# Maxima over partitions by a transpose, a batch norm chain on GpSimd, and weight steps spaced anew in a convolution and attention kernel

## The chip, the cores and the metric

The kernel runs on one core of a Trainium2 chip. A core has a matrix engine (TensorE, PE in the profile; its weight loads are PEld), three engines for element-wise work (VectorE, DVE; ScalarE, ACT; GpSimd, POOL), and a queue engine (SyncE, SP) that issues the transfers here. Each engine works through its own stream of instructions in order, and the streams meet at semaphores. The metric is the device time of one execution in microseconds; lower is better.

## What is computed

The input is x of shape (128, 128, 16, 16), in float32. Layer 0 is a residual block of two quantised convolutions, layer 1 a bidirectional state-space layer and a mixture of experts. The change lies in layer 0:

```python
def _weight_quant(w):                       # 4 bits
    t = jnp.tanh(w)
    t = t / (2.0 * jnp.max(jnp.abs(t))) + 0.5
    return 2.0 * _quantize_k(t, 4) - 1.0
h = _act_quant(_bn(x, gamma1, beta1))       # clip to 0..1, round to 4 bits
out = _conv3x3(h, _weight_quant(w1) * pat1)
out = _act_quant(_bn(out, gamma2, beta2))
out = _conv3x3(out, _weight_quant(w2) * pat2)
return out + x
```

Here x is first group-normalised. `_bn` takes mean and variance of each channel over the whole batch, so the second convolution can't begin before the first has ended for all images. `jnp.max` runs over the whole weight tensor. The pattern `pat1` leaves five of nine taps, a cross, and `pat2` five others, the diagonals.

## The kernel before, in words

Channels lie on the 128 partitions. Images go two at a time, so there are 64 tiles of 128 x 512 (NP = 64). Four stages follow each other.

*Normalisation* (L346 to L474): all 64 tiles of x are loaded once and stay in SBUF (`xr`). VectorE and ScalarE take statistics of each image, and a chain of small VectorE operations makes scale and bias of group norm and first batch norm (`sc1`, `bi1`).

*First convolution* (`conv1`, L477): for each tile, `quantised` makes the 4-bit image: ScalarE (L488) does the scaling with a clip at zero for one image of the pair, GpSimd for the other (L490, and L492 for the clip, every third of which is VectorE's); on six tiles ScalarE does both. VectorE rounds into a padded buffer (L183, `hpad`, four of them, so the stage prepares tiles up to three ahead). TensorE does five matmuls of 512 columns (L210), ScalarE moves the result out of PSUM (L505), VectorE takes statistics (L506), and all but five tiles (`kept`) are stored to HBM (L508).

*Crossover* (L515 to L523): the statistics are aggregated (L516) and turned into scale and bias of the second batch norm (`sc2`, `bi2`). The helper `rsqrt_eps` adds epsilon on VectorE (L124) and takes the power on GpSimd (L127).

*Second convolution* (`conv2`, L532): each tile is fetched (L544), scaled (L548), rounded (L183) and convolved (L210); GpSimd or, for one image of every second pair, ScalarE (L576, L578) scales the residual, VectorE adds it (L579), TensorE transposes the sum into tokens (L557), ScalarE copies that out (L559), and it is stored (L560).

After that come layers 1 and 2, from L590 on, which neither the change nor the steps of the prediction touch.

The weights of a convolution are quantised by `conv_weights` (L132), a generator: each `next` does one step of some 128 x 1152 elements. It needs a maximum over all partitions twice: once of the tanh values (L138, L141), and once (L161, L163) of what is left after a cast to bfloat16, which tells whether one bfloat16 part is enough. Both are `partition_all_reduce` on GpSimd. The answer goes to `how` (L169). `by_weights` (L215) loads `how` into a register of every engine and branches: to a form with nine taps and three parts, one with nine taps and one part, or one with five taps and one part. With these inputs the last one runs, in both convolutions. The steps for the first convolution are spread through the normalisation; those for the second through the loop of the first convolution, one step at every fifth tile from the eighth (L509), with the rest after the loop (L512).

`second_weights` (L299) is another such generator: it prepares weights of the later layers, among them 16 small copies (L326), four products (L328), two centrings of 128 x 512 (L308, L309) and a 512 KB load (L302). `conv2` calls it at every eighth tile.

Instructions are written in the order of the program, but a scheduler orders each engine's stream by priority; `issue_after` ties the instructions of its block behind the one named. Where it is absent, a step whose inputs are ready may be placed far ahead of where it was written.

Of the kernel before, what the change touches and what calls it, by code (L numbers as in the profile page):

```python
# [8 lines left out]
F32 = mybir.dt.float32  # L9
BF16 = mybir.dt.bfloat16  # L10
AF = mybir.ActivationFunctionType
ALU = mybir.AluOpType
AX = mybir.AxisListType

P = 128
NT = 256
EPS = 1e-5
# [3 lines left out]
SCALE = 225.0  # L21
NLEV = 15.0
# [10 lines left out]

@with_exitstack
def kernel(ctx: ExitStack, tc: tile.TileContext, a: dict):
    from concourse import bass_isa

    nc = tc.nc
    x_d, out_d = a["x"], a["out"]
# [89 lines left out]

    CROSS, DIAGONAL = [1, 3, 4, 5, 7], [0, 2, 4, 6, 8]  # L130

    def conv_weights(parts, how, setup, w, pat, taps, tag):  # L132

        t = setup.tile([P, 9, P], F32, name=f"t_{tag}", tag="t")
        nc.scalar.activation(t, w, AF.Tanh)
        yield
        mx = setup.tile([P, 1], F32, name=f"mx_{tag}", tag="mx")
        nc.vector.tensor_reduce(mx, t, AX.XY, ALU.max, apply_absolute_value=True)  # L138
        yield
        am = setup.tile([P, 1], F32, name=f"am_{tag}", tag="am")  # L140
        nc.gpsimd.partition_all_reduce(am, mx, P, bass_isa.ReduceOp.max)  # L141
        yield
        nc.vector.tensor_scalar(am, am, 2.0, None, ALU.mult)
        rm = setup.tile([P, 1], F32, name=f"rm_{tag}", tag="rm")
        nc.vector.reciprocal(rm, am)
        nc.vector.tensor_scalar(t, t, rm, 0.5, ALU.mult, ALU.add)
        yield
        nc.vector.tensor_scalar(t, t, NLEV, MAGIC, ALU.mult, ALU.add)
        yield
        nc.vector.tensor_scalar(t, t, MAGIC, 2.0, ALU.subtract, ALU.mult)  # L150
        yield
        nc.vector.scalar_tensor_tensor(
            w, t, -NLEV, pat.unsqueeze(2).to_broadcast([P, 9, P]), ALU.add, ALU.mult
        )
        yield
        nc.scalar.copy(parts[:, :, 0, :], w)
        yield
        nc.vector.tensor_tensor(t, w, parts[:, :, 0, :], ALU.subtract)
        yield

        nc.vector.tensor_reduce(mx, t, AX.XY, ALU.max, apply_absolute_value=True)  # L161
        yield
        nc.gpsimd.partition_all_reduce(am, mx, P, bass_isa.ReduceOp.max)  # L163
        yield
        nc.vector.tensor_scalar(am, am, 0.0, 2.0, ALU.not_equal, ALU.mult)
        for tap in range(9):
            if tap not in taps:
                nc.vector.scalar_tensor_tensor(am, pat[:, tap : tap + 1], 0.0, am, ALU.not_equal, ALU.max)
        nc.vector.tensor_copy(how, am)  # L169
        nc.scalar.copy(parts[:, :, 1, :], t)  # L170
        nc.gpsimd.tensor_tensor(w, t, parts[:, :, 1, :], ALU.subtract)
        nc.scalar.copy(parts[:, :, 2, :], w)
# [161 lines left out]
    with tc.tile_pool(name="w1p", bufs=1) as w1p:  # L334
# [15 lines left out]
        with tc.tile_pool(name="setup1", bufs=1) as setup, tc.tile_pool(  # L350
# [1 line left out]
        ) as psa:  # L352
            w1 = w1p.tile([P, 9, P], F32, name="w1", tag="w")
            nc.sync.dma_start(w1, a["L0_conv_w1"])
            weights = conv_weights(wq1, how1, w1p, w1, pat1, CROSS, "c1")
            for _ in range(3):
                next(weights)

# [118 lines left out]
        def conv1(taps, nq):  # L477
            with tc.tile_pool(name="pb", bufs=3) as pb, tc.tile_pool(
                name="psb", bufs=4, space=PSUM
            ) as psb:  # L480
                weights = conv_weights(wq2, how2, w1p, w2, pat2, DIAGONAL, "c2")

                def quantised(i):
                    q = pb.tile([P, 2, NT], F32, name=f"q1_{i}", tag="q", bufs=4)
                    for k in range(2):
                        sc, bi = sc1[:, 2 * i + k : 2 * i + k + 1], bi1[:, 2 * i + k : 2 * i + k + 1]
                        if k == 0 or i % 10 == 5:
                            nc.scalar.activation(q[:, k, :], xr[i][:, k, :], AF.Relu, bias=bi, scale=sc)  # L488
                        else:
                            nc.gpsimd.tensor_scalar(q[:, k, :], xr[i][:, k, :], sc, bi, ALU.mult, ALU.add)  # L490
                            eng = nc.vector if i % 3 == 0 else nc.gpsimd
                            eng.tensor_scalar(q[:, k, :], q[:, k, :], 0.0, None, ALU.max)  # L492
                    quantise(q, hpads[i % 4], nq)

                pads(nq)
                less = offsets(pb, psb, wq1, taps, nq)
                for i in range(3):
                    quantised(i)
                for i in range(NP):
                    if i + 3 < NP:  # L500
                        quantised(i + 3)
                    ps = psb.tile([P, 2, NT], F32, name=f"cv1_{i}", tag="cv")
                    conv3x3(ps, hpads[i % 4], wq1, taps, nq)
                    o1 = kept[i] if i in kept else pb.tile([P, 2, NT], F32, name=f"o1_{i}", tag="o1")
                    nc.scalar.activation(o1, ps, AF.Identity, bias=less)  # L505
                    behind = nc.vector.bn_stats(o1st[:, i, :], o1.rearrange("p b s -> p (b s)"))  # L506
                    if i not in kept:
                        nc.sync.dma_start(o1_d[i], o1)  # L508
                    if i > 5 and i % 5 == 3:  # L509
                        with tc.issue_after(behind.ins):  # L510
                            next(weights, None)
                for _ in weights:  # L512
                    pass

                mv2 = pb.tile([P, 2], F32, name="mv2", bufs=1)  # L515
                nc.vector.bn_aggr(mv2, o1st)  # L516
                rs2 = pb.tile([P, 1], F32, name="rs2", bufs=1)
                nc.vector.tensor_scalar(rs2, mv2[:, 1:2], 1.0 / SCALE**2, None, ALU.mult)
                rsqrt_eps(rs2, rs2, EPS)
                nc.vector.tensor_scalar(sc2, rs2, gam2, 1.0 / NLEV, ALU.mult, ALU.mult)  # L520
                tmp2 = pb.tile([P, 1], F32, name="tmp2", bufs=1)
                nc.vector.tensor_tensor(tmp2, mv2[:, 0:1], sc2, ALU.mult)
                nc.vector.scalar_tensor_tensor(bi2, bet2, NLEV, tmp2, ALU.mult, ALU.subtract)  # L523


        kepts = ExitStack()
# [5 lines left out]
    def conv2(taps, nq):  # L532
        with tc.tile_pool(name="pc", bufs=6) as pc, tc.tile_pool(
# [32 lines left out]
            for i in range(NP):  # L566
# [5 lines left out]
                conv3x3(ps, hpads[i % 4], wq2, taps, nq)  # L572
                for k in range(2):
                    sc, bi = ares[:, b + k : b + k + 1], bres[:, b + k : b + k + 1]
                    if k == 0 and i % 2 == 1:
                        nc.scalar.activation(xr[i][:, k, :], xr[i][:, k, :], AF.Identity, bias=bi, scale=sc)  # L576
                    else:
                        nc.gpsimd.tensor_scalar(xr[i][:, k, :], xr[i][:, k, :], sc, bi, ALU.mult, ALU.add)  # L578
                nc.vector.scalar_tensor_tensor(xr[i], ps, less, xr[i], ALU.add, ALU.add)  # L579

                stored(i - 1)
                if i % max(NP // 8, 1) == 0:
                    next(weights, None)
            stored(NP - 1)
            for _ in weights:
                pass
# [617 lines left out]
```

## Time and profile before

| | us |
|---|---|
| time, median of three runs | 2788.83 |
| lowest and highest | 2786.76, 2788.87 |
| span of the profiled execution | 2784.6 |

The span divides as follows, with the busy time of each engine in each stretch, in microseconds.

| stage | from, to | length | PE | DVE | ACT | POOL |
|---|---|---|---|---|---|---|
| normalisation | 0, 77.77 | 77.77 | 5.2 | 58.0 | 42.8 | 14.8 |
| first convolution, first to last matmul | 77.77, 189.53 | 111.76 | 88.0 | 80.3 | 77.8 | 76.3 |
| crossover | 189.53, 203.08 | 13.55 | 0.3 | 8.4 | 5.6 | 5.3 |
| second convolution | 203.08, 320.15 | 117.07 | 115.3 | 76.7 | 90.6 | 55.5 |
| later layers | 320.15, 2784.6 | 2464.45 | 2407.2 | 2109.6 | 1805.5 | 1492.6 |

How to read the profile. A line of a timeline gives the start, the length, the engine, the source line and operation, the tensors and their shapes, the number of instructions merged in it, and in brackets how long the engine had been idle before it, with what ended that wait ("issue": nothing that the profile shows). L-numbers are lines of the kernel. A code such as 128x512 is partitions by elements. The lines of busy shares cut the span into 40 equal slices and give tenths. The two `partition_all_reduce` calls in the first convolution are the lines L141 and L163; the profile gives them 0.38 us each, and custom operations of GpSimd are recorded roughly.

### The profile page before, as it was taken

The numbers are of one execution on the slowest core, as the hardware profiler recorded it, in microseconds if no ns is written. First come the engines' busy times: TensorE is split into PE (matmuls) and PEld (weight loads), VectorE is DVE, ScalarE is ACT, GpSimd is POOL, SyncE is SP. The second block draws the span as 40 slices with busy tenths as digits, with TensorE's granted clock in tenths as the row PEclk, the third lists the DMA queues.
The fourth block names the chain that finished last, engine by engine and source line by source line (L and its number), as shares of the span: only waits on it lengthen the run. The fifth ranks groups of instructions, "written<-read, shape, count | busy, mean of one in ns | idle before, by whom it ended". The sixth has DMA issues, their size and how long they took to land.

```text
span 2784.6 us, 47424 instructions
## 1 busy us (share of the span) xinstructions
PE 2616.0 (94%) x15840; PEld 1667.9 (60%) x15840; DVE 2333.0 (84%) x6226; ACT 2022.2 (73%) x3538; POOL 1644.5 (59%) x1709
## 2 busy tenths in 40 slices
PE   0769679999999999999999999999999999999997
PEld 0225346666666666666666666666666666666664
DVE  7677589888888888898888888888888898888874
ACT  5659577777777777777777777777777777777771
POOL 1667314666566666665665666656666666566566
PEclk9989889999999999999999999999999999999998
DMA  8348501222222232222222222322222222222223
GB/s 269 119 149 283 180 20 55 89 90 93 86 88 78 85 93 86 92 87 88 81 81 86 93 85 93 93 85 84 81 87 93 86 92 86 88 77 79 85 86 106
DMA packets 165415, 275.55 MB, mean 99 GB/s; under 512 B 46240, under 2 KB 89248, under 8 KB 165152
## 3 DMA queue, kind: packets, MB, share of 16 engines
q1 hardware_dynamic: 165152, 272.32, 30.7%
q8 instruction: 131, 2.15, 0.3%
q14 instruction: 132, 1.08, 0.1%
HBM read 197.45 MB, written 58.03 MB: 92 GB/s over the span
## 4 chain that ended last, share of the span: by engine, by line
PE 87%; POOL 1%; ACT 1%; DVE 1%; DMA 1%; issue 1%; POOLq 0%; ACTq 0%; DVEq 0%; SPq 0%
PE f_ps L1079 16%; PE x_ps L794 12%; PE y_ps L918 9%; PE z_ps L837 9%; PE o_ps L967 8%; PE sg L883 4%; PE n_ps L947 4%; PE y_ps L924 4%; PE xt_ps L849 4%; PE g_ps L868 4%; PE dt_ps L704 2%; PE rt_ps L996 2%; PE cv L210 2%; PE sg L885 2%; PE u_ps L686 1%; PE r_ps L754 1%
## 5 line engine op out<-in xcount | busy, mean ns | idle before, releaser
L893 ACT ACTIVATE e<-sg 128x512 f32<-128x512 f32 x768 | 450.2, 595 | 355.6 <-PE sg L883 317.9
L1067 POOL TENSOR_TENSOR gb<-gb,u2T 128x512 f32<-128x512 f32 x512 | 642.4, 1277 | 7.7 <-DMA gb<-gd 7.7
L812 DVE SCALAR_TENSOR_TENSOR xc<-x_ps,cw,xc 128x510 f32<-128x510 f32 (+2 forms) x768 | 569.3, 741 | 82.2 <-ACT xc L806 74.1
L934 POOL TENSOR_TENSOR yg<-yg,z 128x512 f32<-128x512 f32 x256 | 328.0, 1282 | 447.4 <-DVE yg L930 445.5
L1079 PE MATMUL f_ps<-gb,ew 128*128 128x512 f32 x1024 | 522.3, 604 | 5.9 <-POOL gb L1067 5.7
L794 PE MATMUL x_ps<-uT,wx 128*128 128x512 f32 x768 | 404.7, 609 | 7.7 <-DVE bc L812 3.1
L812 DVE SCALAR_TENSOR_TENSOR bc<-x_ps,cw,bc 128x510 f32<-128x510 f32 (+2 forms) x384 | 281.5, 733 | 126.0 <-ACT bc L806 122.5
L918 PE MATMUL y_ps<-e,xt 128*64 128x256 f32 x2048 | 317.7, 389 | 1.1 <-DVE yg L930 1.1
L899 DVE TENSOR_TENSOR e<-e,g_ps 128x1024 f32<-128x1024 f32 x256 | 310.1, 1211 | 2.0 <-ACT e L893 2.0
L837 PE MATMUL z_ps<-uT,wz 128*128 128x512 f32 x512 | 274.5, 618 | 1.4 <-ACT z L841 1.4
L967 PEld LDWEIGHTS o_ps<-wo,yg 128*128 128x128 f32 x2048 | 239.2, 192 | 17.8 <-issue 17.5
L967 PE MATMUL o_ps<-wo,yg 128*128 128x128 f32 x2048 | 249.8, 275 | 0.0
L1079 PEld LDWEIGHTS f_ps<-gb,ew 128*128 128x128 f32 x1024 | 172.7, 192 | 122.0 <-issue 99.7
L841 ACT ACTIVATE z<-z_ps 128x512 f32<-128x512 f32 x256 | 153.3, 599 | 123.1 <-PE z_ps L837 121.3
L806 ACT ACTIVATE xc<-x_ps,cb,cw 128x512 f32<-128x512 f32 x256 | 198.8, 777 | 44.0 <-PE x_ps L794 41.4
L667 POOL TENSOR_TENSOR rstdb<-rstdb,mhalf 128x4 f32<-128x4 f32 x64 | 64.5, 1007 | 280.9 <-DVE rstdb L664 280.9
L930 DVE SCALAR_TENSOR_TENSOR yg<-xc,dcol,y_ps 128x512 f32<-128x512 f32 x256 | 189.1, 739 | 40.4 <-PE y_ps L924 40.1
L210 PE MATMUL cv<-hpad,wq 128*128 128x512 bf16 x640 | 182.0, 430 | 33.9 <-DVE hpad L183 33.9
L957 POOL TENSOR_TENSOR rr<-rr,mhalf 128x8 f32<-128x8 f32 x64 | 105.5, 1648 | 163.0 <-DVE rr L951 163.0
L883 PE MATMUL sg<-rows,cols 128*128 128x256 bf16 x1024 | 196.1, 273 | 5.1 <-ACT e L893 3.4
L924 PE MATMUL y_ps<-e,xt 128*64 128x128 f32 x2048 | 198.8, 273 | 0.0
L883 PEld LDWEIGHTS <-cols 128*128 128x128 bf16 x1024 | 94.9, 98 | 164.5 <-issue 160.8
(244 smaller groups left out, 5292.4 us busy)
## 6 DMA issues: line engine op xcount, KB each, us to landing
gb<-gd SPq DMA_DIRECT2D x256, 512.0 KB
xr<-in_x SPq DMA_DIRECT2D x64, 256.0 KB
y<-yt SPq DMA_DIRECT2D x64, 256.0 KB
yt<-y SPq DMA_DIRECT2D x64, 256.0 KB
cc<-bc SPq DMA_DIRECT2D x128, 128.0 KB
out<-ob SPq DMA_DIRECT2D x64, 256.0 KB
o<-o SPq DMA_DIRECT2D x59, 256.0 KB
q<-o SPq DMA_DIRECT2D x59, 256.0 KB
```

What stands on the lines that cost most here:

```text
L794: nc.tensor.matmul(ps, wx[d][:, n * P : (n + 1) * P], uTs[i], start=True, stop=True)
L812: nc.vector.scalar_tensor_tensor(acc[:, :, to], raw[:, :, of], cw[:, d, n, 3 - back : 4 - back], acc[:, :, to], ALU.mult, ALU.add,)
L837: nc.tensor.matmul(ps, wz[:, d, n * P : (n + 1) * P], uTs[i], start=True, stop=True)
L883: nc.tensor.matmul(sg[:, :, of], c_[:, k, d, s, half, :], r_[:, :, d, t, of], start=True, stop=True)
L893: nc.scalar.activation(e0[:, :, t, :] if j < 2 else e1, sg, AF.Exp)
L899: nc.vector.tensor_tensor(e0.rearrange("p h t l -> p h (t l)"), e0.rearrange("p h t l -> p h (t l)"), gps[i, d, k][:, 0:NT].unsqueeze(1).t ...
L918: nc.tensor.matmul(y_ps[64 * q : 64 * q + 64, k, :], xt[:, 2 * k + s0, 64 * h : 64 * h + 64], e0[:, h].rearrange("p t l -> p (t l)"), star ...
L924: nc.tensor.matmul(y_ps[64 * q : 64 * q + 64, k, s1 * P : (s1 + 1) * P], xt[:, 2 * k + s1, 64 * h : 64 * h + 64], e1[:, h, :], start=False ...
L934: nc.gpsimd.tensor_tensor(yg, yg, zs[i, d][:, n, :], ALU.mult)
L967: nc.tensor.matmul(o_ps[:, (2 * j + d) * P : (2 * j + d + 1) * P], ygs[i, d, n][:, t * P : (t + 1) * P], wo[d][:, n, :], start=(n == 0), s ...
L1067: nc.gpsimd.tensor_tensor(gb[:, e], gb[:, e], u2Ts[i], ALU.mult)
L1079: nc.tensor.matmul(f_ps, ew[:, e, :], gbs[i, e], start=False, stop=(e == NE - 1))
```

## The change

Four edits.

1. The maximum over partitions is taken by TensorE and VectorE: the column of 128 maxima, read as a 128 x 128 matrix by repeating it, is transposed into PSUM, and VectorE takes the maximum along each row. One more PSUM buffer (`mx_ps`) is used for it.
2. The steps of the second convolution's weights go at every fourth tile from the sixth on, instead of at every fifth from the eighth.
3. Scale and bias of the second batch norm are computed by five GpSimd operations instead of five VectorE operations and one of GpSimd.
4. In the second convolution, ScalarE scales the residual of one image in every fourth pair instead of every second (16 images instead of 32; GpSimd takes the others), and the steps of `second_weights` come at the end of each group of eight tiles instead of at its start, tied behind the residual addition of that tile.

```diff
-    def conv_weights(parts, how, setup, w, pat, taps, tag):
+    def conv_weights(parts, how, setup, psums, w, pat, taps, tag):
+        def everywhere(n):
+            mx_ps = psums.tile([P, P], F32, name=f"mx_ps_{tag}{n}", tag="mx_ps", bufs=1)
+            nc.tensor.transpose(mx_ps, mx.to_broadcast([P, P]), ident)
+            nc.vector.tensor_reduce(am, mx_ps, AX.X, ALU.max)
...
-        nc.gpsimd.partition_all_reduce(am, mx, P, bass_isa.ReduceOp.max)
+        everywhere(0)
...
-        nc.gpsimd.partition_all_reduce(am, mx, P, bass_isa.ReduceOp.max)
+        everywhere(1)
...
-                    if i > 5 and i % 5 == 3:
+                    if i > 5 and i % 4 == 2:
                         with tc.issue_after(behind.ins):
                             next(weights, None)
...
-                nc.vector.tensor_scalar(rs2, mv2[:, 1:2], 1.0 / SCALE**2, None, ALU.mult)
-                rsqrt_eps(rs2, rs2, EPS)
-                nc.vector.tensor_scalar(sc2, rs2, gam2, 1.0 / NLEV, ALU.mult, ALU.mult)
+                nc.gpsimd.tensor_scalar(rs2, mv2[:, 1:2], 1.0 / SCALE**2, EPS, ALU.mult, ALU.add)
+                nc.gpsimd.tensor_tensor(rs2, rs2, mhalf[:, 0:1], ALU.pow)
+                nc.gpsimd.tensor_scalar(sc2, rs2, gam2, 1.0 / NLEV, ALU.mult, ALU.mult)
...
-                nc.vector.tensor_tensor(tmp2, mv2[:, 0:1], sc2, ALU.mult)
-                nc.vector.scalar_tensor_tensor(bi2, bet2, NLEV, tmp2, ALU.mult, ALU.subtract)
+                nc.gpsimd.tensor_scalar(tmp2, mv2[:, 0:1], sc2, -1.0, ALU.mult, ALU.mult)
+                nc.gpsimd.tensor_scalar(bi2, bet2, NLEV, tmp2, ALU.mult, ALU.add)
...
-                    if k == 0 and i % 2 == 1:
+                    if k == 0 and i % 4 == 1:
...
-                nc.vector.scalar_tensor_tensor(xr[i], ps, less, xr[i], ALU.add, ALU.add)
+                behind = nc.vector.scalar_tensor_tensor(xr[i], ps, less, xr[i], ALU.add, ALU.add)
...
-                if i % max(NP // 8, 1) == 0:
-                    next(weights, None)
+                if i % max(NP // 8, 1) == max(NP // 8, 1) - 1:
+                    with tc.issue_after(behind.ins):
+                        next(weights, None)
```

More of the change, by code (lines that the diff above doesn't have):

```diff
@@ L35 @@
 def kernel(ctx: ExitStack, tc: tile.TileContext, a: dict):
-    from concourse import bass_isa
     nc = tc.nc
@@ L354 @@
             nc.sync.dma_start(w1, a["L0_conv_w1"])
-            weights = conv_weights(wq1, how1, w1p, w1, pat1, CROSS, "c1")
+            weights = conv_weights(wq1, how1, w1p, psa, w1, pat1, CROSS, "c1")
             for _ in range(3):
@@ L480, in conv1 @@
             ) as psb:
-                weights = conv_weights(wq2, how2, w1p, w2, pat2, DIAGONAL, "c2")
+                weights = conv_weights(wq2, how2, w1p, psb, w2, pat2, DIAGONAL, "c2")
                 def quantised(i):
```

## The prediction

> **What bounds the kernel now.** I began with the page. In the 40 slices of 69.6 us PE is below 9 in five of the first six and in the last, and the granted clock is at 8 in three of those six and in the last.
>
> ```profile
> PE   0769679999999999999999999999999999999997
> DVE  7677589888888888898888888888888898888874
> PEclk9989889999999999999999999999999999999998
> ```
>
> The reader is to see that from the seventh slice on TensorE is full, and that the convolutions, where the change lies, are in the part ahead of it. So I cut the head into stages (busy time by stretch): normalisation 0 to 77.77 us, first convolution to 189.53, crossover to 203.08, second convolution to 320.15, the rest 2464.45. Within the first convolution TensorE works 87.98 of 111.76 us, in the second 115.28 of 117.07. The timeline of PE shows where the missing 23.8 us lie:
>
> ```profile
> 77.77 24.91 PE L210 MATMUL cv<-hpad,wq 128*128 128x512 bf16 x90 [6.63 <-DVE hpad L183]
> 102.97 2.73 PE L210 MATMUL cv<-hpad,wq 128*128 128x512 bf16 x10 [0.29 <-DVE hpad L183]
> 116.52 12.92 PE L210 MATMUL cv<-hpad,wq 128*128 128x512 bf16 x45 [10.82 <-DVE hpad L183]
> ...
> 183.90 5.63 PE L210 MATMUL cv<-hpad,wq 128*128 128x512 bf16 x15 [10.31 <-DVE hpad L183]
> 199.26 0.30 PE L202 MATMUL less_ps<-off,wq 128*128 128x2 bf16 x5 [9.73 <-ACT kept L548]
> 203.08 2.31 PE L210 MATMUL cv<-hpad,wq 128*128 128x512 bf16 x5 [3.52 <-DVE hpad L183]
> ```
>
> Two holes of 10.82 and 10.31 us; all the others in the stage sum to 2.6 us. The named releaser, VectorE's write of the padded image (L183), is only the messenger. The timeline of POOL shows the cause, around the first hole:
>
> ```profile
> 99.23 0.85 POOL L492 TENSOR_SCALAR q<-q 128x256 f32<-128x256 f32 x1
> 106.37 0.38 POOL L141 PARTITION_ALL_REDUCE am_c<-mx_c  x1 [6.29 <-DVE o1st L506]
> 113.67 1.10 POOL L490 TENSOR_SCALAR q<-xr,sc,bi 128x256 f32<-128x256 f32 x2 [6.92 <-issue]
> ```
>
> The reduction is 0.38 us long, but GpSimd stands still for 6.29 us ahead of it and 6.92 us behind it: 13.6 us without a single quantised image. The second one (L163, at 173.96) has 5.98 and 6.89 us. The images in hand carry TensorE on for 5.6 us (100.08 to 105.70), and after GpSimd's restart it takes 2.9 us until the next image is written; so 10.8 of the 13.6 us turn into a hole.
>
> The third place is the crossover, where 12 us pass from the last statistics (190.97) to the first matmul of the second convolution:
>
> ```profile
> 191.01 1.89 DVE L516 BATCH_NORM_AGGREGATE mv<-o1st 128x2 f32<-128x384 f32 x1
> 193.36 0.59 POOL L127 TENSOR_TENSOR rs<-rs,mhalf 128x1 f32<-128x1 f32 x1 [6.13 <-DVE am_c L168]
> 194.12 0.14 DVE L169 CAST how<-am_c 128x1 int32<-128x1 f32 x1
> 194.43 0.16 DVE L523 SCALAR_TENSOR_TENSOR bi<-bet,tmp 128x1 f32<-128x1 f32 x1
> 197.44 3.63 ACT L548 ACTIVATE kept<-kept,bi,sc 128x512 f32<-128x512 f32 x5 [7.19 <-issue]
> 198.33 0.43 DVE L326 COPY dtb<-few_dt_bias 128x8 f32<-128x8 f32 x3 [3.74 <-issue]
> 198.37 0.77 POOL L192 MEMSET hpad<- 128x72 f32 x7 [4.42 <-issue]
> ```
>
> `how`, which chooses the form of the second convolution, is ready only at 194.26, because the last weight step runs at the end of the loop. Every engine loads it and branches: ACT's next work comes 3.2 us later, VectorE's and GpSimd's some 4.1. VectorE then does preparation for later layers (L326, L328, 198.33 to 202.67) ahead of the first image (202.67), and TensorE starts at 203.08.
>
> [...] 5.98 to 6.29 us ahead of the reductions here, and as much again on the way back. [...] Here the loads after 183.90 come every 0.43 us instead of 0.257 as at 160 us, so each hole costs more than its length. [...] Here L578 takes 551 to 1047 ns with a median of 557[...].
>
> **The change, part by part.**
>
> *Reductions by transpose, first convolution.* In the changed kernel's GpSimd stream both reductions and the configuration instructions around them are gone, so both 13 us stalls go. The two holes give 10.82 + 10.31 = 21.1 us. [...] 45 matmuls took 12.92 us instead of 45 x 0.257 = 11.6, and 15 took 5.63 instead of 3.9, together 3.1 us. Added are two transposes on PE (four of L557 take 0.44 us, so 0.11 each) and two VectorE maxima over 128x128 (L464, the same shape from SBUF, 0.29). In PE's stream the transposes stand behind 15 and 46 tiles' matmuls, three or four tiles after the VectorE step that they read, so PE waits for nothing; VectorE reads them behind statistics that wait for the same tile. Bounds 0.8 us (the bare durations) to 3 (each maximum also waiting out a tile's 1.28 us); I take 1.
>
> *Weight steps every fourth instead of every fifth tile.* The same steps in fewer tiles, done by tile 52 instead of after the last. They load VectorE: L146 0.82, L152, L158, L161 1.33 each. By the pace: between the holes 41 tiles took 116.52 to 173.58; less 1.4 us of cold clock that is 1.36 us a tile, with such steps; ahead of the first hole 20 tiles took 27.9 us, less 1.8 cold, 1.305 a tile. So 44 tiles x 1.365 + 20 x 1.305 + 1.8 = 88.0 us for the stage, against 111.8: **23.8 us saved**. Removing the holes alone gives 21.1 + 3.1 - 1 = 23.2; the two agree. The split L171 (2.37 us on GpSimd) now falls at tile 52, mid-loop, where GpSimd may run up to six tiles ahead: hidden. Bounds for the stage: 21.5 to 25.5.
>
> *Crossover.* Only the chain statistics, aggregate, scale and shift, first image stays. From the last statistics T: aggregate to T+1.9; five GpSimd operations, 0.59 for the power and some 0.3 from start to start for the rest (nmr L668 at 339.02, L669 at 339.32), to T+3.9, 0.3 us later than VectorE's chain is now. `how` is long ready, so ACT (its last work ends T-0.7, branch 3.2) and PE (4.75 us as at 70.84, from T-1.4) have branched before. VectorE, free after the aggregate, is through at T+1.9+3.6 = 5.5; ACT's first image at T+4.7, VectorE's write to T+5.9 (the L326 and L328 work now stands behind a tile in mid-loop). GpSimd branches only after the chain: at the first convolution it took 2.58 us (71.11 to 73.69), so T+6.5, and its border memsets, which the first matmul waits for, take 0.45 to that image: T+7.0. Against T+12.1 now: **5.1 us saved**. Bounds: a GpSimd branch of 4.1 us leaves 3.6; memsets hidden under VectorE's write give 6.2.
>
> *Second convolution.* 16 images (L576, 0.59 us) move from ACT to GpSimd (0.557): GpSimd has 112 x 0.62 = 69 us of them in 117. PE idles 1.8 us there; ACT, 90.6 busy, is behind part of that. The weight steps keep their number, but later: the 512 KB bias load leaves the head of SP's queue, where it stood ahead of image fetches; the 20 small VectorE operations (4.3 us) now stand in mid-loop, under three images in hand (5.2 us of PE work). **0.7 us saved**, bounds -2 to 2.
>
> *First stage.* The same transposes there, with 8 us less of waiting for the weights. VectorE idled 1.40, 0.41 and 0.26 us (39.3 to 43.6) on casts and reductions that come earlier now. The last input lands at 57 and VectorE's statistics run to 62.7, so part counts: **1.0 us**, bounds -1 (two transposes waited for at 0.5) to 3.
>
> Sum 23.8 + 5.1 + 0.7 + 1.0 = 30.6. The profiled span is 2784.6, so 2754.0; the runs' median of 2788.83 lies 4.2 above the span, so 2758.2. The layers behind 320 us have the same instruction order and only start earlier.
>
> **Rivals.** *Another engine becomes the bound of the first convolution.* With both holes gone nobody gets time to catch up. GpSimd's pace between 158.50 and 167.41 was six images in 8.91 us, 1.485 each, beside VectorE's two-input step L158; 58 of 64 tiles need one: 1.345 a tile, and more if steps every fourth tile slow it further, up to the full 1.485: 95 us, a gain of 16.7 instead of 23.8, so 2765. For it: GpSimd was 13.9 of 14.5 us busy from 77.7 to 92.2. Against: between the holes it still idled some 5 us.
>
> *The first part does nothing:* the stalls come from something else, such as the stores, and stay. Then crossover and small parts remain, 6.8 us: 2782. Against: DMA is busy 0.14 to 0.23 of the time in the holes, and GpSimd stops exactly there.
>
> *Slower: GpSimd bounds the second convolution.* 112 of its images must pass in the stage. It decides from (117 + 30) / 112 = 1.31 us each, beyond which the loss outweighs the rest; at 1.4 us the stage takes 157, and the total is 2788.8 + 157 - 117 - 29.9 = 2799. The maximum of 1.047 us in 96 and the median of 0.557 speak against it.
>
> **How the numbers follow.** Forecast as summed 0.75; another bound in the first convolution 0.16; nothing from the first part 0.03; slower 0.03; more than all parts' upper bounds allow 0.03. All upper bounds together (25.5 + 6.2 + 2 + 3) gain 36.7, so 2752; all lower ones (21.5 + 3.6 - 2 - 1) gain 22.1, so 2767, which takes in the first rival. A change under 0.2% (5.6 us) could not be told from none. Faster 0.94, within 0.2% 0.03, slower 0.03.
>
> **What would show it.** Right: no stop over 2 us of GpSimd or PE between 77 and the end of the first convolution, which lasts 86 to 90 us; some 8.4 us from its last matmul to the next stage's first, ended by GpSimd's memsets; the second convolution 115 to 118 us; the rest 2464 within 3. Wrong: a pace above 1.42 us a tile with GpSimd or VectorE full; the first matmul of the second convolution waiting on the bias of the batch norm; a rest that changes by more than 5 us.

## The result, and the profile after

| | before | after |
|---|---|---|
| time, median of four runs each, us | 2788.85 | 2761.18 |
| lowest and highest | 2786.76, 2790.59 | 2759.12, 2762.93 |
| span of the profiled execution | 2784.6 | 2758.0 |

The ratio of the times is 0.9901, with a 95% interval of 0.9884 to 0.9918. The forecast was 2758.2. Lines of the changed code stand some six further down: L210 is now L216, L183 is L189, L192 is L198, L505 is L511, L516 is L522, L548 is L554.

Cut at the same events as before, the spans differ by stage as follows.

| stage | before | after | saved | predicted |
|---|---|---|---|---|
| normalisation, to the first matmul | 77.77 | 75.71 | 2.06 | 1.0 |
| first convolution | 111.76 | 88.52 | 23.24 | 23.8 |
| crossover | 13.55 | 11.01 | 2.54 | 5.1 |
| second convolution | 117.07 | 117.26 | -0.19 | 0.7 |
| later layers | 2464.45 | 2465.50 | -1.05 | 0 |
| sum | 2784.6 | 2758.0 | 26.6 | 30.6 |

The spans are those of one profiled execution each; the medians differ by 27.7 us.

On the page, in the 40 slices of now 68.95 us, the second and third of PE (69 to 207 us, the first convolution and the start of the second) read 8 and 8 where they read 7 and 6, and the granted clock of the third is 9 where it was 8:

```profile
PE   0889589999999999999999999999999999999997
PEclk9999799999999999999999999999999999999998
```

The timeline of PE for the same stretch as before has no hole left in the first convolution:

```profile
75.71 19.52 PE L216 MATMUL cv<-hpad,wq 128*128 128x512 bf16 x70 [6.19 <-DVE hpad L189]
96.29 1.44 PE L216 MATMUL cv<-hpad,wq 128*128 128x512 bf16 x5 [1.05 <-DVE hpad L189]
97.57 0.27 PE L137 MATMUL mx_ps_c<-ident,mx_c 128*128 128x128 f32 x1
97.67 27.71 PE L216 MATMUL cv<-hpad,wq 128*128 128x512 bf16 x105
...
138.54 0.27 PE L137 MATMUL mx_ps_c<-ident,mx_c 128*128 128x128 f32 x1
...
152.59 11.63 PE L216 MATMUL cv<-hpad,wq 128*128 128x512 bf16 x45 [0.23 <-DVE how L175]
166.45 0.29 PE L208 MATMUL less_ps<-off,wq 128*128 128x2 bf16 x5 [2.23 <-ACT o L511]
175.24 3.99 PE L216 MATMUL cv<-hpad,wq 128*128 128x512 bf16 x10 [8.50 <-POOL hpad L198]
```

The reader is to see three things. The longest stop of TensorE in the stage is 1.05 us, where two of over 10 us stood. The two transposes (L137) have no bracket: they wait for nothing and are 0.27 us long, and the next matmul starts 0.10 and 0.24 us after they did. And the last line names GpSimd's border memsets (L198) as what the second convolution starts on, as predicted, but the wait before it is longer than predicted. GpSimd's own timeline shows why:

```profile
169.08 0.19 POOL L524 TENSOR_SCALAR rs<-mv 128x1 f32<-128x1 f32 x1 [9.33 <-DVE mv L522]
...
170.76 0.26 POOL L529 TENSOR_SCALAR bi<-bet,tmp 128x1 f32<-128x1 f32 x1
174.72 0.72 POOL L198 MEMSET hpad<- 128x72 f32 x7 [3.70 <-issue]
```

The chain of five operations ends at 171.02, as worked out. Then GpSimd takes 3.70 us over the branch, where 2.58 had been assumed. The timeline of ACT shows a second thing, a wait that the prediction did not have:

```profile
162.99 0.69 ACT L511 ACTIVATE o<-cv,less 128x512 f32<-128x512 f32 x1 [0.59 <-PE cv L216]
165.65 0.69 ACT L511 ACTIVATE o<-cv,less 128x512 f32<-128x512 f32 x1 [1.98 <-DMA o<-o]
171.05 3.63 ACT L554 ACTIVATE kept<-kept,bi,sc 128x512 f32<-128x512 f32 x5 [4.71 <-POOL bi L529]
```

TensorE's last matmul ends at 164.23, but the evacuation of that tile waits 1.98 us for a store, since the buffer that it writes (`o`, one of three) is still being sent to HBM. So the aggregate (L522) starts 2.87 us after the last matmul instead of 1.48 as before.

### The profile page after: what moved, and what is told of

It is laid out like the page before. It is cut to its first block, busy times and chain, and to the rows that moved or that the text cites. A ratio compares the mean times of both kernels' runs of the same rounds, so it can differ in the third digit from the quotient of the medians.

```text
span 2758.0 us, 47416 instructions
## 1 busy us (share of the span) xinstructions
PE 2614.2 (95%) x15844; PEld 1667.5 (60%) x15844; DVE 2342.1 (85%) x6225; ACT 2015.2 (73%) x3522; POOL 1653.0 (60%) x1725
## 3 DMA queue, kind: packets, MB, share of 16 engines
q8 instruction: 131, 2.15, 0.3%
## 4 chain that ended last, share of the span: by engine, by line
PE 89%; DMA 3%; DVE 3%; POOL 2%; ACT 2%; issue 1%; SPq 0%; POOLq 0%; DVEq 0%; ACTq 0%
PE f_ps L1086 16%; PE x_ps L801 12%; PE y_ps L925 9%; PE z_ps L844 9%; PE o_ps L974 8%; PE sg L890 4%; PE n_ps L954 4%; PE y_ps L931 4%; PE xt_ps L856 4%; PE g_ps L875 4%; PE cv L216 4%; PE rt_ps L1003 2%; PE dt_ps L711 2%; PE sg L892 2%; DMA xr<-in_x 2%; PE u_ps L693 1%
## 5 line engine op out<-in xcount | busy, mean ns | idle before, releaser
L216 PE MATMUL cv<-hpad,wq 128*128 128x512 bf16 x640 | 178.7, 423 | 17.8 <-DVE hpad L189 8.9
```

## The experiments

The stages of all kernels, from the timelines of one profiled execution each, in microseconds. "Wait" is from the start of the aggregate to the first matmul of the second convolution, and "branch" is how long GpSimd idles there ahead of its first work behind the branch. In before and in experiments 1, 11 and 12 some 0.3 us of it is a wait for `how`.

| kernel | first conv. | crossover | wait | branch | second conv. | span | median |
|---|---|---|---|---|---|---|---|
| before | 111.76 | 13.55 | 12.07 | 4.42 | 117.07 | 2784.6 | 2788.85 |
| after | 88.52 | 11.01 | 8.14 | 3.70 | 117.26 | 2758.0 | 2761.18 |
| 1 transposes only | 87.49 | 14.78 | 11.99 | 3.94 | 118.21 | 2762.2 | 2763.77 |
| 2 all but transposes | 116.05 | 11.91 | 8.15 | 3.69 | 124.16 | 2796.2 | 2796.91 |
| 3 chain on VectorE | 89.17 | 9.32 | 7.82 | 2.37 | 117.47 | 2757.6 | 2760.61 |
| 4 steps every fifth | 87.04 | 11.54 | 8.75 | 3.10 | 118.77 | 2760.3 | 2760.77 |
| 5 ScalarE's old share | 89.33 | 8.81 | 5.56 | 0.58 | 120.84 | 2761.6 | 2759.89 |
| 6 later weights early | 89.02 | 12.56 | 9.18 | 4.72 | 120.49 | 2762.7 | 2764.28 |
| 7 borders by VectorE | 89.29 | 8.65 | 5.39 | 0.58 | 118.05 | 2756.0 | 2757.81 |
| 8 less unused code | 90.15 | 8.86 | 5.50 | 0.52 | 118.04 | 2757.9 | 2760.30 |
| 9 borders, four buffers | 88.24 | 6.88 | 5.38 | 0.58 | 117.23 | 2751.5 | 2755.93 |
| 10 borders, last tiles kept | 88.82 | 7.02 | 5.53 | 0.58 | 118.99 | 2755.1 | 2757.06 |
| 11 reductions doubled | 138.96 | 13.74 | 12.26 | 4.20 | 117.29 | 2814.0 | 2815.71, one run |
| 12 one doubled, first stage | 113.04 | 13.77 | 12.29 | 4.22 | 116.35 | 2784.7 | 2786.39, one run |

Each kernel was timed beside before on the same chip; the medians of before in those calls lay between 2788.4 and 2789.1.

The layers behind have the same work in all of them and took between 2464.1 and 2467.5 us, so two executions can differ there by up to 3.4 us.

### 1. The transposes alone

Before, with edit 1 only.

```diff
-        nc.gpsimd.partition_all_reduce(am, mx, P, bass_isa.ReduceOp.max)
+        everywhere(0)
...
-        nc.gpsimd.partition_all_reduce(am, mx, P, bass_isa.ReduceOp.max)
+        everywhere(1)
```

> The kernel before with the first edit alone: both maxima over partitions by a transpose, everything else as before. Theory (each of the two stalls of GpSimd in the first convolution [...] ends with the reductions): no stop of PE over 2 us between its first matmul and the last of the first convolution, that stage 86 to 90 us instead of 111.8, first matmul 1 to 2 us earlier, crossover still 12 to 14.5 us, the span 23 to 26 us below before. Rival (the stalls belong to the stores or to VectorE and stay): the stage stays near 110 us and the span within 3 us of before.

Measured: 2763.77 us, ratio 0.9909 (0.9892 to 0.9925). In its timeline of PE the first transpose stands in the stream without a wait:

```profile
99.37 0.27 PE L136 MATMUL mx_ps_c<-ident,mx_c 128*128 128x128 f32 x1
99.47 1.43 PE L215 MATMUL cv<-hpad,wq 128*128 128x512 bf16 x5
101.28 45.00 PE L215 MATMUL cv<-hpad,wq 128*128 128x512 bf16 x175 [0.37 <-DVE hpad L188]
```

The first convolution takes 87.49 us. The first matmul of the second still comes 12 us after the start of the aggregate; the crossover as a whole, 14.78 us, is 1.2 us longer than before, since the aggregate starts 2.8 us after the last matmul instead of 1.5. So one edit of four brings 25.2 of the 27.7 us (by the profiled spans 22.4 of 26.6), and the cause is the one named: with the reductions gone from GpSimd, the holes are gone.

### 2. Everything but the transposes

After, with the two reductions back on GpSimd.

```diff
-        everywhere(0)
+        nc.gpsimd.partition_all_reduce(am, mx, P, bass_isa.ReduceOp.max)
...
-        everywhere(1)
+        nc.gpsimd.partition_all_reduce(am, mx, P, bass_isa.ReduceOp.max)
```

> The changed kernel with the two reductions put back on GpSimd, so the other three edits alone. Theory: both stalls are back, the first convolution 110 to 114 us, and the crossover as in the changed kernel, 10 to 12 us from the last matmul to the next stage's first; the span 1 to 5 us below before. Rival (the nearer spacing of steps or the moved chain brings a good part by itself): the span 8 us or more below before.

Measured: 2796.91 us, ratio 1.0029 (1.0018 to 1.0041): slower than before, where a gain was expected. The timeline of PE has its two holes again:

```profile
112.81 6.80 PE L211 MATMUL cv<-hpad,wq 128*128 128x512 bf16 x20 [9.51 <-DVE hpad L184]
...
172.84 8.65 PE L211 MATMUL cv<-hpad,wq 128*128 128x512 bf16 x25 [12.08 <-DVE hpad L184]
```

The holes sum to 21.6 us, against 21.1 before, so they do not explain the loss. The crossover is indeed shorter, by 1.6 us; but the first convolution is 4.3 us longer, and the second 7.1. In the second, PE was busy 117.8 us instead of 115.3, and idle 6.3 instead of 1.8 (the mean granted clock of the stage was 0.96, against 0.98). The largest stop there begins with a fetched tile that comes late, in the timelines of ACT and of PE:

```profile
249.54 0.81 ACT L549 ACTIVATE q<-q,bi,sc 128x512 f32<-128x512 f32 x1 [2.16 <-DMA q<-o]
```

```profile
251.38 0.66 PE L558 MATMUL yt_ps<-ident,xr 128*128 128x128 f32 x4 [1.42 <-ACT yt L560]
```

ScalarE waits 2.16 us for its tile and so gets late to the results of the transposes, for which TensorE then waits. With the transposes in place the same code in the second convolution takes 117.26. Why it is so much worse in this kernel was not settled; what the run shows is that edits 2 to 4 together gain nothing without the first.

### 3. The chain back on VectorE

After without edit 3.

```diff
-                nc.gpsimd.tensor_scalar(rs2, mv2[:, 1:2], 1.0 / SCALE**2, EPS, ALU.mult, ALU.add)
-                nc.gpsimd.tensor_tensor(rs2, rs2, mhalf[:, 0:1], ALU.pow)
-                nc.gpsimd.tensor_scalar(sc2, rs2, gam2, 1.0 / NLEV, ALU.mult, ALU.mult)
+                nc.vector.tensor_scalar(rs2, mv2[:, 1:2], 1.0 / SCALE**2, None, ALU.mult)
+                rsqrt_eps(rs2, rs2, EPS)
+                nc.vector.tensor_scalar(sc2, rs2, gam2, 1.0 / NLEV, ALU.mult, ALU.mult)
...
-                nc.gpsimd.tensor_scalar(bi2, bet2, NLEV, tmp2, ALU.mult, ALU.add)
+                nc.vector.scalar_tensor_tensor(bi2, bet2, NLEV, tmp2, ALU.mult, ALU.subtract)
```

> The changed kernel with scale and bias of the second batch norm back on VectorE (power on GpSimd), nothing else. Theory (in the changed kernel GpSimd branches only after the chain and its border memsets come last; on VectorE the chain delays VectorE's branch by as much): GpSimd branches 1.3 us earlier, VectorE 1.6 us later and its first image comes 7.4 to 8 us after the last statistics, so the first matmul moves by -0.7 to +0.3 us and the time stays within 1 us. Rival (the move to GpSimd is what shortens the crossover): the crossover is 2 us or more longer than in the changed kernel.

Measured: 2760.61 us, ratio 0.9901 (0.9884 to 0.9917), the wait 7.82 against 8.14. Edit 3 is worth nothing that can be measured. The operations take about the same time on either engine (1.7 us from the end of the aggregate on VectorE, 2.0 on GpSimd), and the branch comes behind them on both: here it is VectorE that idles 3.70 us and starts its first image at 173.62, when GpSimd's memsets have been done since 172.29. The crossover is 1.7 us shorter for another reason. The last evacuation waited 0.61 us for TensorE and not for a store, though there were three buffers here too.

### 4. The steps at every fifth tile again

After without edit 2.

```diff
-                    if i > 5 and i % 4 == 2:
+                    if i > 5 and i % 5 == 3:
```

> The changed kernel with the weight steps at every fifth tile from the eighth, as before, so that the form of the second convolution is known only after the loop again. Theory (the nearer spacing slows the loop by about 1 us, and since GpSimd branches last in any case, a late answer hardly lengthens the crossover): first convolution 87 to 88.3 us, first matmul of the second 8 to 9.5 us after the last statistics, span within 1.5 us of the changed kernel. Rival (the early answer is what shortens the crossover): that distance 11 us or more, the span 2.5 us or more above the changed kernel.

Measured: 2760.77 us, ratio 0.9896 (0.9879 to 0.9912). The late answer costs the crossover 0.6 us (8.75 against 8.14), and the first convolution is 1.5 us shorter (87.04 against 88.52). Over all kernels without holes, the two with steps at every fifth tile took 87.0 and 87.5 us, the eight with every fourth 88.2 to 90.2. So this edit seems to give with one hand and take with the other.

### 5 and 6. The two halves of edit 4

After, with ScalarE scaling every second pair's first image again:

```diff
-                    if k == 0 and i % 4 == 1:
+                    if k == 0 and i % 2 == 1:
```

> The changed kernel with ScalarE scaling 32 residual images in place of 16. Theory (the second convolution is held by PE with transfers close behind, and what ScalarE is relieved of it spends waiting for fetched tiles): that stage 116 to 118.3 us against 117.3, ScalarE's waits for fetched tiles fall back from 18.9 to 8 to 13 us. Rival (ScalarE held the stage and the relief was eaten up by GpSimd or the later weight steps): the stage grows by 2 us or more.

And after, with the steps of `second_weights` at the start of each group of eight tiles again, untied:

```diff
-                if i % max(NP // 8, 1) == max(NP // 8, 1) - 1:
-                    with tc.issue_after(behind.ins):
-                        next(weights, None)
+                if i % max(NP // 8, 1) == 0:
+                    next(weights, None)
```

> The changed kernel with the weights of the later layers prepared as before: at the start of each group of eight tiles and free to be placed earlier. Theory (GpSimd's branch and border memsets set the first matmul, and the 4.3 us of small VectorE work fit ahead of that): VectorE does L326 and L328 ahead of the first image again, and the first matmul moves by 0 to 1 us. Rival (keeping this work out of the head is a good part of the gain): the first matmul moves by 3 to 4.5 us.

Measured: 2759.89 us (ratio 0.9894, 0.9877 to 0.9910) and 2764.28 (0.9914, 0.9897 to 0.9930). Neither interval parts from the one of after. The second convolution got longer in both profiled executions, 120.84 and 120.49 us against 117.26. For experiment 5 that is beyond the 118.3 of its theory, and it is what its rival had named as its sign. Its profiled execution was also the slowest of its four (2763.35, the others 2756.93 to 2760.34), so the size is uncertain.

In the crossover of experiment 5, which got 2.2 us shorter, GpSimd's branch took 0.58 us instead of 3.70. Nobody had expected that, and it led to experiments 7 and 8. In experiment 6 the wait grew by 1.0 us, the most that its theory allowed. There the 512 KB load stands second in the queue of transfers again (at 171.33 us), where in after it comes behind the first six fetches (at 173.69); whether that is what lengthens the second convolution is not shown.

What edit 4 as a whole moved is seen in the waits of ACT over the second convolution, of before and of after (the total in us, how often, the longest):

```profile
ACT q L548 <- DMA q<-o: 10.0, 14, 1.7
```

```profile
ACT q L554 <- DMA q<-o: 18.9, 21, 2.2
```

ScalarE has 5.9 us less work (84.7 against 90.6 busy) and waits 8.9 us more for fetched tiles. TensorE is busy 115.1 of 117.3 us in that stage, so there were 2 us to gain at most. In experiment 5 ScalarE is busy 94.0 us and its waits for tiles are 10.4, as the theory said; but TensorE idles 4.8 us instead of 2.2, mostly for ScalarE's copies of the transposed sums (L565). So against before the edit gains nothing in this stage, and yet, in that execution, ScalarE's larger share was not free beside the later weight steps. Either half of the edit taken back alone lengthens the stage by over 3 us, and edits 2 to 4 taken back together (experiment 1) by 1; why is not settled.

### 7. The borders by VectorE

After, with the border memsets of the second convolution on VectorE instead of GpSimd.

```diff
-    def pads(nq):
+    def pads(nq, eng):
-                nc.gpsimd.memset(at, HALF if nq == 1 else 0.0)
+                eng.memset(at, HALF if nq == 1 else 0.0)
...
-            pads(nq)
+            pads(nq, nc.vector)
```

> The changed kernel with the border memsets of the second convolution on VectorE in place of GpSimd. Theory (GpSimd's branch after the chain is the last gate): the first matmul comes 5.2 to 6 us after the last statistics in place of 8.2, the crossover 8 to 9 us in place of 11.0, the span 1.5 to 3 us below the changed kernel. Rival (another gate, PE's own branch or ScalarE's image, is just behind): the first matmul moves by less than 1 us.

Measured: 2757.81 us, ratio 0.9894 (0.9878 to 0.9911). The wait falls from 8.14 to 5.39 us and the crossover from 11.01 to 8.65. But GpSimd's branch also took 0.58 us here, so that the memsets may not have needed moving at all: this run alone can't tell a shorter way from a faster branch.

### 8. Less code that never runs

The run before takes memsets out of three forms of the second convolution, of which only one is executed. So here they are left out of the two nine-tap forms alone, which these inputs never reach (there the borders would be missing).

```diff
-            pads(nq)
+            if len(taps) < 9:
+                pads(nq)
```

> After, with the border memsets left out in the two nine-tap forms of the second convolution, which these inputs never execute: 16 GpSimd instructions fewer stand between the branch and the code it jumps to, and nothing that runs is changed. Theory (GpSimd's time for the branch [...] depends on where the target lies): GpSimd's branch falls from 3.7 us to about 0.6, as in the run with the borders on VectorE, and the first matmul comes 5.4 to 5.9 us after the start of the aggregate, not 8.1, with the memsets still on GpSimd; the time falls by about 2 us, to 2759 or so. Rival (what helped there was that the memsets were taken off GpSimd): the branch stays at 3.1 to 4 us and the first matmul at 8 us, the time at 2761.

Measured: 2760.30 us, ratio 0.9899 (0.9882 to 0.9915), and GpSimd's timeline in the crossover:

```profile
172.48 0.26 POOL L529 TENSOR_SCALAR bi<-bet,tmp 128x1 f32<-128x1 f32 x1
173.26 0.72 POOL L198 MEMSET hpad<- 128x72 f32 x7 [0.52 <-issue]
```

```profile
174.32 1.89 PE L216 MATMUL cv<-hpad,wq 128*128 128x512 bf16 x4 [5.86 <-DVE hpad L189]
```

With not one executed instruction changed, the branch takes 0.52 us instead of 3.70, the wait is 5.50 us, and TensorE starts on VectorE's image. So the 3 us depend on code that never runs and not on what the executed code does; the theory's reading, that it is where the code lies, fits but is not shown by itself. Each figure is from one execution, but they recur where the second convolution's code is the same: 3.70 in after and 3.69 in experiment 2, 0.58 in experiments 7, 9 and 10. Since the memsets are back on GpSimd and the wait is still within 0.1 us of that in experiment 7, moving them was worth next to nothing.

The total hardly follows: the crossover is 2.15 us shorter, but this execution's first convolution is 1.6 us longer with the same instructions, and its store wait (2.47 us) too.

### 9 and 10. The store that holds the last buffer

Both have the borders on VectorE. The first gives the results of the first convolution four buffers instead of three:

```diff
-                    ... else pb.tile([P, 2, NT], F32, name=f"o1_{i}", tag="o1")
+                    ... else pb.tile([P, 2, NT], F32, name=f"o1_{i}", tag="o1", bufs=4)
```

> After, with the borders of the second convolution on VectorE and four buffers for the results of the first convolution instead of three. Theory (the last result waits for a store that still holds its buffer): the wait of the last tile's ScalarE evacuation falls from 2 us to under 0.7, the aggregate starts about 1.5 us after the last matmul, the crossover takes 7 to 7.5 us instead of 8.65 with the borders alone, and the span falls by a further 1 to 1.5 us, to 2754.5 to 2755. Rival (the store queue itself is behind, so a fourth buffer is used up as well): the wait stays above 1.5 us, and nothing changes against the run with the borders alone.

The second keeps other tiles in SBUF, the last three among them:

```diff
-        kept = {i: ... for i in range(min(NKEPT, NP // 4))}
+        kept = {i: ... for i in (0, 1, NP - 3, NP - 2, NP - 1)}
```

> As the run with the borders on VectorE, but the five tiles that are never stored are 0, 1, 61, 62 and 63 instead of 0 to 4, so the last three results need neither a store nor one of the three buffers. Theory: no wait for a store ahead of the last evacuation, aggregate about 1.5 us after the last matmul, crossover about 7 us; the three stores of tiles 2 to 4 come early in the stage, where they have time, but their fetches come early in the second convolution, which may cost up to 1 us there. Span 2753.5 to 2755.5. Rival (the end of the first convolution was not held up by stores): crossover 8.5 us or more, as in the run with the borders alone.

Measured: 2755.93 us (ratio 0.9885, 0.9868 to 0.9901) and 2757.06 (0.9886, 0.9869 to 0.9902). In the timelines of the first, ACT and then PE:

```profile
163.29 0.69 ACT L511 ACTIVATE o<-cv,less 128x512 f32<-128x512 f32 x1 [0.59 <-PE cv L216]
168.69 3.63 ACT L554 ACTIVATE kept<-kept,bi,sc 128x512 f32<-128x512 f32 x5 [4.72 <-POOL bi L529]
```

```profile
164.47 0.29 PE L208 MATMUL less_ps<-off,wq 128*128 128x2 bf16 x5 [1.22 <-ACT o L511]
170.12 4.21 PE L216 MATMUL cv<-hpad,wq 128*128 128x512 bf16 x10 [5.36 <-DVE hpad L189]
```

The last evacuation now waits for its matmul and no longer for a DMA. In both kernels the aggregate starts 1.5 us after the last matmul, and the crossover takes 6.88 and 7.02 us. So the wait was for the buffer, and one more buffer, or results that need none, removes it. It is not there in every kernel with three: ahead of the last evacuation it was 1.98 to 2.48 us in after and in experiments 5 to 8, 1.00 in experiments 1 and 4, and none in experiment 3. What sets it was not tested. The kernel with four buffers has the shortest span of all, 6.5 us below after: 4.1 of that is the crossover, and the rest is spread over the other stages as between repeats. Its profiled execution was the fastest of its four; the medians are 5.2 us apart. Its interval still overlaps that of after.

### 11 and 12. What the two reductions paid for

Before, with each reduction of the second convolution's weights issued twice in a row:

```diff
         nc.gpsimd.partition_all_reduce(am, mx, P, bass_isa.ReduceOp.max)
+        if tag == "c2":
+            nc.gpsimd.partition_all_reduce(am, mx, P, bass_isa.ReduceOp.max)
```

> The kernel before with each reduction over partitions of the second convolution's weights issued twice in a row, so four in place of two, with the same result. Theory ([...] once in and once out around the pair): each pair stops GpSimd for 13.5 to 15 us, hardly longer than one call, and the span grows by 0 to 2 us. Rival (each call costs its 13 us by itself, hidden in the rough record of custom operations): each pair stops GpSimd for some 20 to 27 us and the span grows by 14 to 26 us.

Measured: 2815.71 us in a single run, span 2814.0. GpSimd's timeline:

```profile
104.68 0.38 POOL L141 PARTITION_ALL_REDUCE am_c<-mx_c  x1 [6.00 <-DMA o<-o]
111.83 1.09 POOL L494 TENSOR_SCALAR q<-xr,sc,bi 128x256 f32<-128x256 f32 x2 [6.78 <-issue]
112.90 0.88 POOL L496 TENSOR_SCALAR q<-q 128x256 f32<-128x256 f32 x1
119.64 0.38 POOL L143 PARTITION_ALL_REDUCE am_c<-mx_c  x1 [5.86 <-issue]
127.07 1.09 POOL L494 TENSOR_SCALAR q<-xr,sc,bi 128x256 f32<-128x256 f32 x2 [7.05 <-issue]
```

The time rose by some 27 us, at the far end of what the rival had named. But the scheduler had put image work between the two calls, so they were not in a row, and the run could not tell "per call" from "per change of work". It shows only that a reduction with ordinary work on both sides cost 5.86 to 6.00 us ahead and 6.78 to 7.05 us behind, both times. The pair was therefore tried again in the first stage, where GpSimd has nothing to put between:

```diff
+        if tag == "c1":
+            am2 = setup.tile([P, 1], F32, name=f"am21_{tag}", tag="am2", bufs=2)
+            nc.gpsimd.partition_all_reduce(am2, mx, P, bass_isa.ReduceOp.max)
```

> Before, with the second reduction over partitions of the first convolution's weights doubled, in the first stage, where GpSimd has nothing else to put between the two calls; the second result is used by nobody. Theory (the 6 us ahead of a reduction and the 7 us behind it [...] not at each call): the second call starts within 1.5 us of the first, and the idle time of about 6 us stands ahead of the first alone. Rival (each call pays): the second starts 6 to 14 us after the first. The time may rise by 0 to 2 us with the theory and by up to 14 with the rival.

Measured: 2786.39 us in a single run, and in GpSimd's timeline:

```profile
42.86 0.38 POOL L166 PARTITION_ALL_REDUCE am_c<-mx_c  x1 [6.17 <-DVE bst L414]
43.15 0.42 POOL L169 PARTITION_ALL_REDUCE am_c<-mx_c  x1
```

The second call starts 0.29 us after the first, so it has no 6 us of its own ahead of it, and the first no 7 us behind it. The profile of before also lists two configuration instructions (MODIFY_POOL_CONFIG, 11 to 15 ns each) on the line of each of its four reductions, which stand alone; this run has one instruction more than before in all (47425 against 47424), so the second call seems to have none. So the 13 us go with the change from ordinary work to a reduction and back, and not with each call. This rests on one execution and on the profile's rough record of such operations, and the way back is not seen in it: GpSimd's next work comes 27 us later, when its input is ready.

## Why the prediction was right, and where its sizes were off

*First convolution: right.* Predicted 88.0 us for the stage, measured 88.52; the price of the holes held, and so did that of the slower matmuls after them. Behind the two holes of before, the granted clock was 0.50 from 116.52 to 119.7 us and from 183.90 to 187.9, and 1.00 for the rest of the same two stretches of matmuls. TensorE's busy time in the stage fell from 87.98 to 85.37 us although two transposes of 0.27 us came in, 3.1 us less for the same matmuls, as predicted, and the mean granted clock rose from 0.91 to 1.00. The added transposes and maxima hid behind other work. The transposes alone gave 87.49 us.

*Another engine as the bound: did not come.* GpSimd was busy 76.7 of 88.5 us, and the longest stops were 1.05 us of TensorE and 1.30 of GpSimd. *The first part does nothing* fell with the first experiment (over the two holes themselves the DMA engines were busy 0.13 of the time, a little less than the prediction read), and *slower, by GpSimd in the second convolution* with the stage's 117.26 us.

*Crossover: right in its mechanism, off in two terms.* It was said to end on GpSimd's memsets, and it did: VectorE's first image was written at T+5.3 (predicted 5.9), long before them. Here T is the end of the last statistics. Counted from it (167.06), the aggregate ended at T+1.93 (predicted 1.9), the chain at T+3.96 (3.9), and the first matmul came at T+8.18 (7.0). The first term that was mis-sized is GpSimd's branch, taken as 2.58 us from the first convolution: its memsets came 3.70 us after the chain, 1.1 more. The second term is T itself: the last statistics were assumed as far behind the last matmul as before, 1.44 us, and came 2.83 us behind it, since the evacuation waited for a store. The two, 1.1 and 1.4, are nearly the whole difference between 5.1 and 2.54. The 2.54 lies below the lower bound of 3.6, which allowed for a branch of 4.1 us and had nothing for a store. The experiment with four buffers shows the second by taking it away (1.5 us again), and the one with less unused code shows the first (0.52 us).

*Why the store is late now and was not before* was not tested by itself. Before, a hole of 10.3 us ended 5.6 us ahead of the end of the stage, in which no result was made and stores could land; without holes the last results come at TensorE's pace of one in 1.28 us. Experiment 2 fits: it has both holes, but the second ended 21 us ahead of the end of the stage, and the last evacuation waited 1.25 us for a store. Experiment 3, without holes and without the wait, shows that this is not all. It remains an argument.

*Weight steps and later weights: needed together, worth little one by one.* The crossover's 5.1 us rested on `how` being ready early and on the later weights' work being out of the way. Alone taken back, the spacing costs 0.6 us there and the place of the chain nothing. The early preparation of later weights costs 1.0, and that is GpSimd's branch again (4.72 us instead of 3.70): VectorE began to write its images at 173.47, well ahead of the memsets at 176.46. But with all of them as before (the transposes alone) the wait is 3.9 us longer than after. There `how` is ready at 168.93, VectorE's next work comes at 173.06, and the later weights' operations hold back its first image until 177.20. So they overlap: each alone is hidden, or nearly, by GpSimd's branch, and only together do they matter.

*Second convolution:* 0.7 predicted, -0.2 measured, inside its bounds. The 512 KB load left the head of the queue only for the seventh place, ahead of the first matmul, and not for mid-loop. *First stage:* 2.06 instead of 1.0, inside its bounds too. Its size is not sure: with the reductions there, the first matmul came at 76.50 to 78.25 us (before and experiments 2, 11 and 12), with the transposes at 75.00 to 76.03 (the other ten). So the 1.06 us more than predicted, which made up for part of the crossover, are in part luck. *Later layers:* 1.05 us longer, less than kernels with the same work there differ by (2464.1 to 2467.5).

## What to carry to other kernels

A single library call on GpSimd between ordinary operations cost some 36 times its recorded length here (13.6 us for 0.38), and the idle time stood on both sides of it, under no name: look at what that engine did not do, and move such a call to where the engine has nothing else, next to another of its kind, or to another engine. When a stall that kept a pipeline slack is removed, look at what had used the slack: here, it seems, the stores had, and a fourth buffer took their wait away. And where three small edits come with a large one, try each alone: here the large one brought 25.2 of 27.7 us, and the other three together, without it, cost 8 us against before.

## What the runs showed of the hardware that was not expected

GpSimd's idle time around a taken branch lay between 0.52 and 4.72 us in these kernels, for the same load of `how` and the same kind of jump. Leaving 16 instructions out of code that never runs moved it from 3.70 to 0.52. The longer branches, of 2.37 to 4.72 us, took 1.9 to 4.2 us more than the shortest. What GpSimd waits for in that time is not shown. The profile counts transfers of instructions on queues of their own, two in after's 3.70 us (0.02 MB) and six in before's 4.42 (0.06 MB), but it does not say which engine they serve.

The runs do not give the rule: the kernel before has as few GpSimd instructions per form of the second convolution as experiment 5, and still took 4.42 us (0.3 of it the wait for `how`) where that took 0.58. Whether the distance of the jump decides, or how long the engine had stood still, or something else, stays open.

The idle time around a reduction on GpSimd goes with the change and not with the call. In the first convolution, for the two calls of before and the two shown of experiment 11, it was 5.86 to 6.29 us on the way in and 6.78 to 7.05 on the way back; from one reduction to the next, where nothing lies between, it was 0.29 us from start to start (experiment 12). In the four calls shown both were paid every time, and the way back took longer than the way in. What they are paid for is not shown; the profile shows the idle time and the configuration instructions.
